# Inverse deviations and inverse lengths of a two-layer kernel: a root and a reciprocal, or a sum and a power on POOL

## The chip, the cores and the metric

The kernel runs on one core of one Trainium2 chip. A core has five engines with instruction queues of their own, each worked off in order: TensorE (PE, with its weight loads as PEld), VectorE (DVE), ScalarE (ACT), GpSimd (POOL) and SyncE (SP). Engines wait for each other on semaphores. The metric is the device time of one execution in microseconds (us), all of it: two layers of a small sequence model, 8 sequences of 512 tokens with 128 channels, in float32.

## The reference, cut to what matters

Every block is preceded by a normalisation with mean and deviation over the 128 channels (`_layernorm`), and adds its result to `x`.

```python
def _layernorm(x, axis=-1, eps=1e-05):
    m = jnp.mean(x, axis=axis, keepdims=True)
    v = jnp.var(x, axis=axis, keepdims=True)
    return (x - m) / jnp.sqrt(v + eps)
...
x = x + _L0_attn_ref(_layernorm(x, axis=-1), ...)
x = x + _L0_ffn_ref(_layernorm(x, axis=-1), ...)
x = x + _L1_attn_ref(_layernorm(x, axis=-1), ...)
x = x + _L1_ffn_ref(_layernorm(x, axis=-1), ...)
```

Inside the blocks there are more inverse roots. The first attention divides each query and key of 8 numbers (16 heads) by its length, and normalises its output:

```python
q = _l2norm((x @ Wq).reshape(b, s, nh, d))
k = _l2norm((x @ Wk).reshape(b, s, nh, d))
...
state = state * (1.0 - bb * kk) + bb * (vt[..., :, None] * kt[..., None, :])
out_t = jnp.einsum('bhij,bhj->bhi', state, qt)
...
out = (out - mu) / jnp.sqrt(var + LN_EPS) * ln_g + ln_b
```

The second attention normalises its input once more, divides each head of its output by the root of its mean square, and normalises again ahead of a small feed-forward part:

```python
h = _ln(x, ln_w, ln_b)
...
o = _rms(o, rms_w) * (g * jax.nn.sigmoid(g))
x = x + o.reshape(Bb, Tt, HEADS * DV) @ Wo
h2 = _ln(x, ln_w, ln_b)
return x + jax.nn.gelu(h2 @ W1 + b1, approximate=False) @ W2 + b2
```

Both feed-forward blocks are mixtures of experts: a router chooses 2 of 8 experts in the first layer and 4 of 16 in the second.

## The kernel before, in words

A batch is one sequence: `x_b` is a tile of 128 partitions by 4 times 128 channels (token 128 t + p lies in partition p, block t). A deviation is thus a number for each token: [128 x 4] for a batch. A length is one for each token and head: 128 x 4 x 32 numbers for queries and keys.

The work has five stages.

1. First attention and first router, for all eight batches (chains `attend0` and `route`, run by the planner at line 918). Tokens of a routed batch are scattered to DRAM row by row by POOL (line 839, eight indirect DMAs for each batch).
2. The eight experts of the first layer, in a fixed order (lines 937 to 970).
3. Second attention, its feed-forward part and second router (chain `attend`), again for eight batches; sixteen indirect DMAs for each batch (line 1413).
4. The sixteen experts of the second layer over 36 groups of four tiles of rows (`fetch`, `prepare`, `first`, `second`).
5. The sum of the four expert results into `x` and the store (lines 1629 to 1638).

In stages 1 and 3 the order of the instructions on each engine is found by a planner when the program is built. A chain is a generator; `yield ACT, 0.35, "sqrt"` says that the next instructions run on ACT, take 0.35 us, and need the table of that name. The planner (`Order.run`, line 143) always takes the step that can begin first by its own clock, on a tie the one with the lower rank (the lower batch). It knows that an engine does one thing at a time, a hop of 0.2 us between engines, and 1.3 us for a change of ACT's table. A chain also waits for signals of other chains and for buffers out of rings. Where PE would idle for more than 0.35 us by the planner's clock, it puts in fills: matmuls into a bank that nobody reads (line 907). The engines then run these lists in order, each instruction as soon as its semaphores allow. What the planner does not know is real: how long transfers take, and what other work an engine has outside the chains, such as the constants that POOL loads at the start (lines 188 to 326).

What the change touches:

- `statistics` (line 426): moments of `x` on DVE, root on ACT (436), reciprocal (438) and shift (439) on DVE, for batch 0, batches 1 and 2, and batches 3 to 7.
- `attend0`: sums of squares of queries and keys come out of PSUM at line 592, are inverted at 593, the root is taken by ACT at 598. Lines 601 and 602 make the factors `f`: [0:16] is (1 + th) / length squared of the key, [16:32] is (1 + th) / length of the key, [32:48] is 1 / length of the query; `th` is the tanh half of beta's sigmoid (595). The factors are transposed by PE (606), copied by ACT (609), and spread over the channels (613, 548, 502); keys, queries and values are multiplied with them (617, 551, 505).
- The recurrence runs on DVE in two groups of four numbers for each batch, over [128 x 2048]: products at 646, 652 and 662 and a scan at 658. ACT makes 1 - product at 626. The keys and queries for it are stored to DRAM and read back spread over partitions (lines 479 and 554).
- `deviation` (line 676): mean square of the result out of PSUM, root on ACT (687), reciprocal on DVE (690), used at 709.
- `route` (line 716): moments, root (725), reciprocal (727), shift (728), normalised rows on ACT (732).
- `attend`: three normalisations, called u, m and g, with roots at 1087 and 1088, at 1255, and at 1298, and the common `shifts` (line 1059, reciprocal at 1062); the head norm with its sum at 1222, root at 1224 and reciprocal at 1226.

Five batches of stage 3 may be in flight (`FLIGHT = 5`), four of stage 1.

Of the kernel before, what the change touches and what calls it, by code (L numbers as in the profile page):

```python
# [9 lines left out]
F32 = mybir.dt.float32  # L10
# [24 lines left out]
DV = 8  # L35
# [26 lines left out]
PE, DVE, ACT, POOL, SP = "PE", "DVE", "ACT", "POOL", "SP"  # L62
# [107 lines left out]
def two_layers(ctx: ExitStack, tc: tile.TileContext, a: dict, out: bass.AP):  # L170
    nc = tc.nc

    const = ctx.enter_context(tc.tile_pool(name="const", bufs=1))
# [35 lines left out]
    nc.gpsimd.affine_select(  # L209
        out=before, in_=ones, pattern=[[1, P]], compare_op=ALU.is_gt, fill=0.0, base=0, channel_multiplier=-1  # L210
    )
    eps = const.tile([P, 1], F32, name="eps")
    nc.vector.memset(eps, EPS)
    eps2 = const.tile([P, 1], F32, name="eps2")
    nc.vector.memset(eps2, EPS * EPS)
    over_c = const.tile([P, 1], F32, name="over_c")
    nc.vector.memset(over_c, 1.0 / C)
    center = const.tile([P, P], F32, name="center")
# [55 lines left out]
    ps = bank_ring.idle[0][2]  # L274
# [122 lines left out]
    mv_a = const.tile([P, B, NT, 2], F32, name="mv_a")  # L397
# [14 lines left out]
    def chunk(t2, t):  # L412
        return t2[:, t * P : (t + 1) * P]

    def affine(dst, src, rs, sh):
        for t in range(NT):
            nc.scalar.activation(
                dst[:, t, :], src[:, t, :], AF.Identity, bias=sh[:, t : t + 1], scale=rs[:, t : t + 1]
            )

    def landing(us):
        s = Signal()
        s.set(order.later(us))
        return s

    def statistics(first, last):

        yield landing(3.0 + first)
        for b in range(first, last):
            yield DVE, 1.75  # L430
            for t in range(NT):
                nc.vector.bn_stats(st_a[:, t, :], xs[b][:, t, :])
                nc.vector.bn_aggr(mv_a[:, b, t, :], st_a[:, t, :])
        yield ACT, 0.35, "sqrt"
        rs, sh = rs_a[:, first:last, :], sh_a[:, first:last, :]
        nc.scalar.activation(rs, mv_a[:, first:last, :, 1], AF.Sqrt, bias=eps)
        yield DVE, 0.4
        nc.vector.reciprocal(rs, rs)
        nc.vector.scalar_tensor_tensor(sh, mv_a[:, first:last, :, 0], -1.0, rs, ALU.mult, ALU.mult)
        for b in range(first, last):  # L440
            have_stats[b].set(order.now)

    def attend0(b):
# [3 lines left out]
        m = yield flight  # L447
# [3 lines left out]
        ps = yield bank_ring  # L451
# [112 lines left out]
        ps = yield bank_ring  # L564
# [17 lines left out]
        ps = yield bank_ring  # L582
# [5 lines left out]
        used_xT()  # L588
        sq_ring.give(order.now, *sq)
        by_kind = ps[:, : NT * 3 * NH].rearrange("p (t n) -> p t n", t=NT)  # L590
        yield DVE, 1.3
        nc.vector.tensor_scalar_max(m.norms, by_kind[:, :, 0 : 2 * NH], 1e-24)
        nc.vector.reciprocal(m.norms, m.norms)
        yield ACT, 0.25, "silu"
        nc.scalar.activation(m.th, by_kind[:, :, 2 * NH :], AF.Tanh, scale=0.5)
        bank_ring.give(order.now, ps)
        yield ACT, 0.4, "sqrt"
        nc.scalar.activation(m.f[:, :, NH:], m.norms, AF.Sqrt)

        yield DVE, 0.45  # L600
        nc.vector.scalar_tensor_tensor(m.f[:, :, 0:NH], m.th, 1.0, m.norms[:, :, 0:NH], ALU.add, ALU.mult)
        nc.vector.scalar_tensor_tensor(m.f[:, :, NH : 2 * NH], m.th, 1.0, m.f[:, :, NH : 2 * NH], ALU.add, ALU.mult)
        ps = yield bank_ring
        yield PE, 0.6
        for t in range(NT):
# [5 lines left out]
        ps = yield bank_ring  # L611
# [64 lines left out]
        def deviation():  # L676
            sq = yield sq_ring
            yield ACT, 0.65
            nc.scalar.activation(sq, acc, AF.Square)
            gone.set(order.now)  # L680
            ps = yield bank_ring
            yield PE, 0.7
            for t in range(NT):
                nc.tensor.matmul(ps[:, t : t + 1], lhsT=chunk(sq, t), rhs=over_c, start=True, stop=True)
            sq_ring.give(order.now, sq)
            yield ACT, 0.3, "sqrt"
            nc.scalar.activation(m.rs_o, ps[:, :NT], AF.Sqrt, bias=eps)
            bank_ring.give(order.now, ps)
            yield DVE, 0.15
            nc.vector.reciprocal(m.rs_o, m.rs_o)  # L690
            have_rs.set(order.now)

        order.add(b, deviation())
# [5 lines left out]
        ps = yield bank_ring  # L699
# [16 lines left out]
    def route(b):  # L716

        x_b = xs[b]
        m = yield routed
        yield DVE, 1.75  # L720
        for t in range(NT):
            nc.vector.bn_stats(m.st[:, t, :], x_b[:, t, :])
            nc.vector.bn_aggr(m.mv[:, t, :], m.st[:, t, :])
        yield ACT, 0.3, "sqrt"
        nc.scalar.activation(m.rs, m.mv[:, :, 1], AF.Sqrt, bias=eps)
        yield DVE, 0.3
        nc.vector.reciprocal(m.rs, m.rs)
        nc.vector.scalar_tensor_tensor(m.sh, m.mv[:, :, 0], -1.0, m.rs, ALU.mult, ALU.mult)
        rw_b = yield rows_ring
        yield ACT, 2.3  # L730
        for t in range(NT):
# [4 lines left out]
                bias=m.sh[:, t : t + 1],  # L736
                scale=m.rs[:, t : t + 1],
            )
        ps = yield bank_ring
# [20 lines left out]
        ps = yield acc_ring  # L760
# [59 lines left out]
        ps = yield bank_ring  # L820
# [233 lines left out]
    def moments(m, src, which):  # L1054
        for t in range(NT):
            nc.vector.bn_stats(m.st[:, t, :], src[:, t, :])
            nc.vector.bn_aggr(m.mv[which][:, t, :], m.st[:, t, :])

    def shifts(m, which, n):

        mv, rs, sh = m.mv[which], m.rs[which], m.sh[which]
        nc.vector.reciprocal(rs, rs)
        mean = mv[:, :, 0].unsqueeze(1).to_broadcast([P, n, NT]) if n > 1 else mv[:, :, 0].unsqueeze(1)
        nc.vector.scalar_tensor_tensor(sh, mean, -1.0, rs, ALU.mult, ALU.mult)

    def attend(b):
# [10 lines left out]
        m = yield flight  # L1077
# [5 lines left out]
        yield DVE, 1.75  # L1083
        moments(m, x_b, "u")

        yield ACT, 0.6, "sqrt"
        nc.scalar.activation(m.rs["u"][:, 0, :], m.mv["u"][:, :, 1], AF.Sqrt, bias=eps)
        nc.scalar.activation(m.rs["u"][:, 1, :], m.mv["u"][:, :, 1], AF.Sqrt, bias=eps2, scale=1.0 + EPS)
        yield DVE, 0.35
        shifts(m, "u", 2)  # L1090

        u = yield u_ring
# [16 lines left out]
        ps = yield bank_ring  # L1109
# [33 lines left out]
        ps = yield bank_ring  # L1143
# [76 lines left out]
        nc.scalar.activation(o, tiled(acc), AF.Square)  # L1220
        yield DVE, 0.7
        nc.vector.tensor_reduce(m.rr, o.rearrange("p t (h d) -> p (t h) d", d=DV), AX.X, ALU.add)
        yield ACT, 0.35, "sqrt"
        nc.scalar.activation(m.rr, m.rr, AF.Sqrt, bias=eps, scale=1.0 / DV)
        yield DVE, 1.3
        nc.vector.reciprocal(m.rr, m.rr)
        nc.vector.tensor_mul(
            o.rearrange("p t (h d) -> p (t h) d", d=DV),
            tiled(acc).rearrange("p t (h d) -> p (t h) d", d=DV),
# [3 lines left out]
        ps = yield bank_ring  # L1233
# [10 lines left out]
        ps = yield bank_ring  # L1244
# [6 lines left out]
        bank_ring.give(order.now, ps)  # L1251
        yield DVE, 1.75
        moments(m, u, "m")
        yield ACT, 0.3, "sqrt"
        nc.scalar.activation(m.rs["m"][:, 0, :], m.mv["m"][:, :, 1], AF.Sqrt, bias=eps)
        yield DVE, 0.35
        shifts(m, "m", 1)
        hn = yield hn_ring
        yield ACT, 1.65
        affine(hn, u, m.rs["m"][:, 0, :], m.sh["m"][:, 0, :])  # L1260
        ps = yield bank_ring
# [18 lines left out]
        ps = yield bank_ring  # L1280
# [13 lines left out]

        yield DVE, 1.75
        moments(m, x_b, "g")
        yield ACT, 0.3, "sqrt"
        nc.scalar.activation(m.rs["g"][:, 0, :], m.mv["g"][:, :, 1], AF.Sqrt, bias=eps)
        yield DVE, 0.35
        shifts(m, "g", 1)  # L1300
        rw_b = yield rows_ring
        yield ACT, 2.95
        for t in range(NT):
# [14 lines left out]
        ps = yield bank_ring  # L1318
# [52 lines left out]
        ps = yield bank_ring  # L1371
# [304 lines left out]
```

## Time and profile before

| | us |
|---|---|
| median of three runs | 1202.57 |
| lowest and highest | 1201.56, 1208.95 |
| profiled execution, its own time | 1211.52 |
| its span, first to last instruction | 1209.8 |

Busy time in that span: PE 943.3, PEld 680.0, DVE 658.2, ACT 474.7, POOL 448.0 us. ACT loads a table 81 times, at 1283 ns each: 33 times in stage 1, 47 in stage 3, once in stage 4.

| stage | from | to |
|---|---|---|
| 1 first attention and router | 0 | 404 |
| 2 first experts | 404 | 497 |
| 3 second attention and router | 497 | 894 |
| planning of the second experts, last scatters | 894 | 913 |
| 4 second experts | 913 | 1170 |
| 5 sum and store | 1170 | 1210 |

How to read it: a line of the timeline gives start, duration, engine, line of the kernel, operation, what is written from what with shapes, and in brackets how long the engine had been idle and what ended that. A line of the waits gives who waited for whom, the total, the number of times and the longest. In the table by stage each row gives the stretch, its length, then for PE, PEld, DVE, ACT and POOL the busy time with the number of instructions, then TensorE's granted clock, the share of the DMA engines and GB/s. "remote" and "issue" are idle times for which the profile shows no engine and no transfer as the cause.

### The profile page before, as it was taken

How to read it: one execution, taken by the hardware profiler on the slowest of the kernel's cores; microseconds unless marked ns; L12 is line 12 of the kernel's file. 1: busy time of each engine (PE TensorE's matmuls, PEld its weight loads, DVE VectorE, ACT ScalarE, POOL GpSimd, SP SyncE). 2: the span in 40 equal slices, each digit the busy share in tenths (PEclk: the TensorE clock that was granted, in tenths of full speed). 3: DMA queues.
4: the chain of work that ended last, by engine and by line, in shares of the span. 5: the costliest groups of instructions: out<-in, count | busy, mean ns of one | idle time of the engine just before them, and what ended most of it. 6: DMA issues, size and time to landing. Idle time of an engine off the chain costs nothing. (4 is left out here: it accounts for less than half of the span.)

```text
span 1209.8 us, 16157 instructions
## 1 busy us (share of the span) xinstructions
PE 943.3 (78%) x4923; PEld 680.0 (56%) x4923; DVE 658.2 (54%) x1628; ACT 474.7 (39%) x892; POOL 448.0 (37%) x459
## 2 busy tenths in 40 slices
PE   7989999997988499689977977977646778768620
PEld 5656566664657266555644544644535677757520
DVE  5478889777962011367766856654342333434317
ACT  4623664733432022272932843623402334333310
POOL 8000045314334234210055145134442656655543
PEclk8887888877977699889987978978867888888765
DMA  7866667585400200340012001001002222222228
GB/s 173 208 151 151 158 162 184 153 202 133 112 6 3 72 15 10 107 146 1 1 36 79 10 27 36 12 25 36 32 31 70 78 75 81 81 74 79 71 80 274
DMA packets 76438, 103.79 MB, mean 86 GB/s; under 512 B 12404, under 2 KB 58358, under 8 KB 72256
## 3 DMA queue, kind: packets, MB, share of 16 engines
q1 hardware_dynamic: 56576, 72.55, 23.4%
q0 software_dynamic: 14832, 27.84, 8.0%
q10 hardware_dynamic: 4944, 2.37, 0.7%
q8 instruction: 40, 0.66, 0.2%
q14 instruction: 46, 0.38, 0.1%
HBM read 69.63 MB, written 37.99 MB: 89 GB/s over the span
## 5 line engine op out<-in xcount | busy, mean ns | idle before, releaser
L839 POOL DMA_INDIRECT row<-rows,si x64 | 92.3, 1442 | 275.8 <-DVE kT L617 144.9
L1413 POOL DMA_INDIRECT rows<-rows,si x128 | 126.3, 986 | 166.0 <-DVE tmp L1390 69.1
L1597 POOL DMA_INDIRECT res<-qy,to x144 | 141.3, 981 | 118.4 <-DVE qw L1558 55.2
L1576 ACT ACTIVATE qh<-mid,cols 128x128 f32<-128x128 f32 x288 | 86.2, 365 | 144.0 <-PE qT L1553 59.8
L907 PEld LDWEIGHTS idle_bank<-ones,ident 128*128 128x128 f32 x956 | 130.9, 214 | 17.3 <-issue 14.6
L907 PE MATMUL idle_bank<-ones,ident 128*128 128x128 f32 x956 | 136.9, 299 | 3.3 <-POOL ident masks.py:199 1.5
L1568 PE MATMUL mid<-dT,qw 128*128 128x128 f32 x576 | 88.0, 315 | 7.9 <-issue 5.9
L1595 DVE TENSOR_TENSOR qy<-qyp,de 128x512 f32<-128x512 f32 x36 | 24.8, 690 | 127.3 <-PE qT L1553 54.3
L1568 PEld LDWEIGHTS mid<-dT,qw 128*128 128x128 f32 x576 | 84.2, 230 | 9.9 <-issue 7.7
L1587 PE MATMUL qyp<-fw,qh 128*128 x576 | 80.4, 291 | 11.8 <-issue 11.7
L1587 PEld LDWEIGHTS qyp<-fw,qh 128*128 128x128 f32 x576 | 75.4, 207 | 13.5 <-issue 12.5
L635 PE MATMUL acc<-add,center 128*128 128x512 f32 x128 | 68.4, 684 | 17.8 <-DVE add L662 17.6
L1553 PE MATMUL qT<-ident,de 128*128 128x128 f32 x144 | 33.2, 311 | 50.4 <-DMA de<-rows 35.1
L658 DVE TENSOR_TENSOR_SCAN add<-dec,add 128x2048 f32<-128x2048 f32 x16 | 70.8, 4424 | 0.6
L1558 DVE COPY qw<-fw 128x256 f32 x144 | 46.2, 336 | 22.8 <-DMA rows<-rows,si 9.8
L635 PEld LDWEIGHTS acc<-add,center 128*128 128x128 f32 x128 | 26.9, 220 | 50.3 <-issue 28.9
L963 POOL DMA_INDIRECT res<-y,de x32 | 31.3, 977 | 62.7 <-DVE y L957 55.4
L1553 PEld LDWEIGHTS qT<-ident,de 128*128 128x128 f32 x144 | 19.2, 149 | 62.2 <-issue 32.8
L943 ACT ACTIVATE hT<-mid,cols 128x512 f32<-128x512 f32 x32 | 22.0, 687 | 75.4 <-PE mid L940 50.8
L1103 POOL TENSOR_TENSOR x<-x,b 128x512 f32<-128x512 f32 x8 | 10.6, 1321 | 109.1 <-DVE u L1098 92.4
L662 DVE TENSOR_TENSOR add<-add,qb 128x2048 f32<-128x2048 f32 x16 | 36.6, 2288 | 23.9 <-DMA qb<-queries 23.6
L1186 PEld LDWEIGHTS acc<-ident,st 128*128 128x128 f32 x256 | 37.4, 216 | 20.3 <-issue 11.3
(338 smaller groups left out, 1949.6 us busy)
## 6 DMA issues: line engine op xcount, KB each, us to landing
add<-keys SPq DMA_DIRECT2D x16, 1024.0 KB
qb<-queries SPq DMA_DIRECT2D x16, 1024.0 KB
de<-rows SPq DMA_DIRECT2D x144, 65.0 KB
yk<-res SPq DMA_DIRECT2D x8, 1024.0 KB
res<-zeros POOLq DMA_DIRECT2D x8, 512.0 KB
ew_all<-in_L_ffn_ew_dram SPq DMA_DIRECT2D x16, 256.0 KB
ys<-res SPq DMA_DIRECT2D x8, 512.0 KB
fw<-in_L_ffn_w_dram SPq DMA_DIRECT2D x32, 128.0 KB
```

Of the source, the lines that this page charges most:

```text
L635: nc.tensor.matmul(acc, lhsT=center, rhs=st[:, j, :], start=g + j == 0, stop=(g + 1) * J + j == D + J - 1)
L658: nc.vector.tensor_tensor_scan(flat, dec.rearrange("p j t -> p (j t)"), flat, 0.0, ALU.mult, ALU.add)
L839: nc.gpsimd.indirect_dma_start(out=row0_w[(b * NT + t) * 2 + k], out_offset=bass.IndirectOffsetOnAxis(ap=m.si[:, t, k : k + 1], axis=0), i ...
L907: nc.tensor.matmul(idle_bank[:, 0:P], lhsT=ident, rhs=ones, start=True, stop=True)
L1186: nc.tensor.matmul(acc[:, t * P : (t + 1) * P], lhsT=st[:, t * P : (t + 1) * P], rhs=ident, start=j + t == 0, stop=j + t == DK + NT - 2,)
L1413: nc.gpsimd.indirect_dma_start(out=rows1_w[(b * NT + t) * K1 + k], out_offset=bass.IndirectOffsetOnAxis(ap=m.si[:, t, k : k + 1], axis=0), ...
L1553: nc.tensor.transpose(ps[:, i * P : (i + 1) * P], de[q][:, i, 0:C], ident)
L1558: nc.vector.tensor_copy(w1_q[:, i, :], fw1[:, bass.ds(at, I1)])
L1568: nc.tensor.matmul(mid[c][:, here], lhsT=w1_q[:, i, c * P : (c + 1) * P], rhs=dT[:, here], start=True, stop=True)
L1576: nc.scalar.activation(hT[:, c, here], mid[c][:, here], AF.Gelu, bias=cols[:, bass.ds(at + c, 1)])
L1587: nc.tensor.matmul(ps[:, here], lhsT=hT[:, c, here], rhs=fw2[:, bass.ds(at + c * C, C)], start=c == 0, stop=c == NC1 - 1,)
L1597: nc.gpsimd.indirect_dma_start(out=res1_w[4 * q + i], out_offset=bass.IndirectOffsetOnAxis(ap=to[:, i : i + 1], axis=0), in_=y[:, i, :], i ...
```

## The change

Every inverse root is taken on POOL as (a + more) to the power of -0.5, with at most two instructions: a sum (or a product and a sum) with numbers, and a power whose exponent is a constant column. ACT takes no square root any more, and DVE inverts none of these. [...]DVE brings them out first: the maximum at 592 as before, and at 687 a sum with EPS in place of ACT's root. The key's factor with the squared length is now made by a product with the inverse length once more, and (1 + th) / length is copied into its place. The planner's entries are changed along with it.

```diff
+    minus_half = const.tile([P, 1], F32, name="minus_half")
+    nc.vector.memset(minus_half, -0.5)
...
+    def root(dst, src, factor, more):
+
+        if factor == 1.0:
+            nc.gpsimd.tensor_scalar_add(dst, src, more)
+        else:
+            nc.gpsimd.tensor_scalar(dst, src, factor, more, ALU.mult, ALU.add)
+        power(dst, dst)
+
+    def power(dst, src):
+        half = minus_half
+        while len(half.shape) < len(src.shape):
+            half = half.unsqueeze(1)
+        nc.gpsimd.tensor_tensor(dst, src, half.to_broadcast(list(src.shape)), ALU.pow)
...
-        yield ACT, 0.35, "sqrt"
+        yield POOL, 0.7
         rs, sh = rs_a[:, first:last, :], sh_a[:, first:last, :]
-        nc.scalar.activation(rs, mv_a[:, first:last, :, 1], AF.Sqrt, bias=eps)
-        yield DVE, 0.4
-        nc.vector.reciprocal(rs, rs)
+        root(rs, mv_a[:, first:last, :, 1], 1.0, EPS)
+        yield DVE, 0.25
...
-        yield DVE, 1.3
+        yield DVE, 0.3
         nc.vector.tensor_scalar_max(m.norms, by_kind[:, :, 0 : 2 * NH], 1e-24)
-        nc.vector.reciprocal(m.norms, m.norms)
...
-        yield ACT, 0.4, "sqrt"
-        nc.scalar.activation(m.f[:, :, NH:], m.norms, AF.Sqrt)
+        yield POOL, 0.8
+        power(m.f[:, :, NH:], m.norms)
 
         yield DVE, 0.45
-        nc.vector.scalar_tensor_tensor(m.f[:, :, 0:NH], m.th, 1.0, m.norms[:, :, 0:NH], ALU.add, ALU.mult)
-        nc.vector.scalar_tensor_tensor(m.f[:, :, NH : 2 * NH], m.th, 1.0, m.f[:, :, NH : 2 * NH], ALU.add, ALU.mult)
+        r_k = m.f[:, :, NH : 2 * NH]
+        nc.vector.scalar_tensor_tensor(m.th, m.th, 1.0, r_k, ALU.add, ALU.mult)
+        nc.vector.tensor_mul(m.f[:, :, 0:NH], m.th, r_k)
+        nc.vector.tensor_copy(r_k, m.th)
...
-            yield ACT, 0.3, "sqrt"
-            nc.scalar.activation(m.rs_o, ps[:, :NT], AF.Sqrt, bias=eps)
+            yield DVE, 0.15
+            nc.vector.tensor_scalar_add(m.rs_o, ps[:, :NT], EPS)
             bank_ring.give(order.now, ps)
-            yield DVE, 0.15
-            nc.vector.reciprocal(m.rs_o, m.rs_o)
+            yield POOL, 0.4
+            power(m.rs_o, m.rs_o)
...
-        yield ACT, 0.3, "sqrt"
-        nc.scalar.activation(m.rs, m.mv[:, :, 1], AF.Sqrt, bias=eps)
-        yield DVE, 0.3
-        nc.vector.reciprocal(m.rs, m.rs)
+        yield POOL, 0.6
+        root(m.rs, m.mv[:, :, 1], 1.0, EPS)
+        yield DVE, 0.2
...
-        yield ACT, 0.6, "sqrt"
-        nc.scalar.activation(m.rs["u"][:, 0, :], m.mv["u"][:, :, 1], AF.Sqrt, bias=eps)
-        nc.scalar.activation(m.rs["u"][:, 1, :], m.mv["u"][:, :, 1], AF.Sqrt, bias=eps2, scale=1.0 + EPS)
-        yield DVE, 0.35
+        yield POOL, 1.0
+        root(m.rs["u"][:, 0, :], m.mv["u"][:, :, 1], 1.0, EPS)
+        root(m.rs["u"][:, 1, :], m.mv["u"][:, :, 1], 1.0 + EPS, EPS * EPS)
+        yield DVE, 0.2
         shifts(m, "u", 2)
...
-        yield ACT, 0.35, "sqrt"
-        nc.scalar.activation(m.rr, m.rr, AF.Sqrt, bias=eps, scale=1.0 / DV)
-        yield DVE, 1.3
-        nc.vector.reciprocal(m.rr, m.rr)
+        yield POOL, 0.8
+        root(m.rr, m.rr, 1.0 / DV, EPS)
+        yield DVE, 0.7
```

The roots of m and g change as that of u does, with one `root` each in place of ACT's root (`yield POOL, 0.6`), and `shifts` loses its reciprocal.

More of the change, by code (lines that the diff above doesn't have):

```diff
@@ L211, in two_layers @@
     )
[L212 to L215, printed above, removed]
+    minus_half = const.tile([P, 1], F32, name="minus_half")
+    nc.vector.memset(minus_half, -0.5)
     over_c = const.tile([P, 1], F32, name="over_c")
@@ L1061, in shifts @@
         mv, rs, sh = m.mv[which], m.rs[which], m.sh[which]
-        nc.vector.reciprocal(rs, rs)
         mean = mv[:, :, 0].unsqueeze(1).to_broadcast([P, n, NT]) if n > 1 else mv[:, :, 0].unsqueeze(1)
@@ L1253, in attend @@
         moments(m, u, "m")
-        yield ACT, 0.3, "sqrt"
-        nc.scalar.activation(m.rs["m"][:, 0, :], m.mv["m"][:, :, 1], AF.Sqrt, bias=eps)
-        yield DVE, 0.35
+        yield POOL, 0.6
+        root(m.rs["m"][:, 0, :], m.mv["m"][:, :, 1], 1.0, EPS)
+        yield DVE, 0.2
         shifts(m, "m", 1)
@@ L1296, in attend @@
         moments(m, x_b, "g")
-        yield ACT, 0.3, "sqrt"
-        nc.scalar.activation(m.rs["g"][:, 0, :], m.mv["g"][:, :, 1], AF.Sqrt, bias=eps)
-        yield DVE, 0.35
+        yield POOL, 0.6
+        root(m.rs["g"][:, 0, :], m.mv["g"][:, :, 1], 1.0, EPS)
+        yield DVE, 0.2
         shifts(m, "g", 1)
```

## The prediction

> **What bounds the kernel now.** I began with the page's first two parts and then cut the execution by stage, at the times where the first and last instruction of each stage's lines start. The table of busy time by stage, one row for each stretch (length, then busy time of PE, PEld, DVE, ACT, POOL with the number of instructions):
>
> ```profile
> 0.00:404.00 404.00, 350.16 (x1619) 242.07 (x1619) 282.12 (x596) 181.14 (x276) 124.35 (x131) 0.83 0.56 134
> 404.00:497.00 93.00, 86.78 (x455) 60.89 (x456) 11.07 (x16) 23.28 (x33) 30.66 (x32) 0.94 0.13 36
> 497.00:894.00 397.00, 317.84 (x1543) 204.68 (x1541) 243.13 (x712) 182.85 (x294) 125.80 (x132) 0.88 0.13 41
> 913.00:1170.00 257.00, 185.52 (x1296) 170.67 (x1296) 91.94 (x251) 87.47 (x289) 140.79 (x144) 0.84 0.26 71
> ```
>
> The edit lies in the first and third rows. PE looks busiest there, but 136.9 us of its time are the fills of L907, put where PE would idle. In the first stage the worker is DVE: from 57 to 366 us it is busy 247.6 of 309 us. In the third nothing is full (DVE 61%, ACT 46%, POOL 32%): chains of eight batches, five in flight, bound it. The chain that ended last reaches back only to about 907 us, so it says nothing of these two stages; the waits do. Table loads of ACT (line, count, busy time, mean ns):
>
> ```profile
> L598 ACT ACT_TABLE_LOAD x8 | 10.3, 1283 | 0.1
> L687 ACT ACT_TABLE_LOAD x3 | 3.8, 1283 | 0.1
> L1224 ACT ACT_TABLE_LOAD x6 | 7.7, 1283 | 0.1
> L1298 ACT ACT_TABLE_LOAD x6 | 7.7, 1283 | 0.1
> ```
>
> and DVE's longest waits in the first stage (waiter, awaited, total us, times, longest):
>
> ```profile
> DVE add L662 <- DMA qb<-queries: 23.6, 5, 8.3
> DVE lg L779 <- PE acc L765: 18.9, 3, 15.0
> DVE dec L656 <- ACT dec L626: 12.3, 4, 5.8
> ```
>
> ACT makes DVE wait for little: 12.3 us on `dec`, some 5 us elsewhere. That is the first warning that 68 us of loads are not 68 us of time.
>
> **What the Trainium skill says.** "ScalarE: Activation LUTs", What ACT_TABLE_LOAD costs: about 1283 ns a load and a drain of some 1380 ns. The trace agrees on the load (1283); the next ACTIVATE follows within 0.02 us, so I use 1.283 alone. "SBUF — State Buffer", Who interferes with whom: a DVE instruction with two SBUF inputs and a POOL instruction that reads SBUF exclude each other for the whole instruction. The trace shows both directions. The scatter that starts 1.1 us into a DVE scan takes 4.11 us instead of 0.98, and a shift of 0.17 us takes 1.00 beside POOL's add:
>
> ```profile
> 162.69 4.42 DVE L658 TENSOR_TENSOR_SCAN add<-dec,add 128x2048 f32<-128x2048 f32 x1
> 163.79 4.11 POOL L839 DMA_INDIRECT row<-rows,si  x1 [0.30 <-issue]
> ...
> 515.29 1.58 POOL L1103 TENSOR_TENSOR x<-x,b 128x512 f32<-128x512 f32 x1 [1.32 <-ACT h1T L1115]
> 515.89 1.00 DVE L1064 SCALAR_TENSOR_TENSOR sh_u<-mv_u,rs_u 128x8 f32<-128x8 f32 x1
> ```
>
> "GPSIMD Engine Reference", Elementwise, prices a two-input add at 2.6 cycles an element and gives no price for a power; L1103 (512 elements, 1.27 to 1.31 us undisturbed) fits the add.
>
> **The change part by part.** *Removed from ACT*: the changed program's order has 28 table loads for 81; 31 fewer in the first stage (33 to 2), 22 in the third (47 to 25). 53 x 1.283 = 68 us. The roots go too: 8 x (0.31 + 0.27 + 0.30) = 7 us in the first stage, 8 x (0.29 + 0.28 + 0.35 + 0.30 + 0.30) = 12 us in the third. ACT falls from 181 to about 134 and from 183 to about 143 us, beside the path wherever ACT waited anyway: several loads were issued while ACT still waited for its data (L1298: load at 755.47, root at 761.04).
>
> *Removed from and added to DVE*: first stage, 8 x (0.953 + 0.161 + 0.163) = 10.2 us of reciprocals; added 8 x 0.18 (sum out of PSUM, nearest row L828) and 8 x 0.20 (a copy of 64 elements, nearest L815 and L893) = 3.0. Net -7. Third stage, 8 x (0.547 + 0.192 + 0.165 + 0.158) = -8.5.
>
> *Added to POOL*: a power, not in the trace. Below, a POOL instruction of this size costs no less than the iota (0.16 to 0.28). Above, I let a power cost ten times the add per element (1.28/512 x 10 = 25 ns, an estimate): 3.2 us for 128 elements. I take the planner's own entries in the diff (0.8 for 128, 0.4 for 4, 0.2 for the sum), since its other entries match the trace (POOL 1.3 against 1.32 for L1103). That is 16.5 us in the first stage and 24 in the third, on a POOL that is busy 124 and 126 us.
>
> *The start.* The first root now stands in POOL's queue behind its constant loads, whose last begins at 19.47; before, ACT had it at 6.25. Working on: root about 20.6, shift 20.9, normalisation to 22.6, transposes, copy at about 24.0, against 18.77: +5. Then four loads (32.42, 33.96, 36.36, 39.80) vanish: -5. The first `kT` product stays at 44 to 45, but the second batch's factors come directly behind the first's, so its keys and queries leave earlier and DVE has work in the 8.3 us stall before 65.67: -4.
>
> *The middle* (57 to 366): DVE's work -6, half of its waits for `dec` -6. The lock: 8 x 1.8 us of POOL roots against a DVE that spends some 181 us of the stage (16 x 11.3) in instructions with two SBUF inputs. Half of a root on 60% of occasions delays DVE: 4 us; the dependent shift or factor that finds its root locked out behind a scan or product costs about 0.5 us for each batch: 4 more. Sum -4. *Its tail*: two loads in front of `rs_o` (356.31, 357.83) vanish: -3. First stage: -11.
>
> *The third stage*: DVE -8.5, half on the path: -4. DVE's waits for ACT there (o 14.3, gk 4.3, gate 4.2, rr 3.9) are 27 us; ACT loses a fifth of its load, and half of these waits: -12. Against that stands the queue. Scatters of one batch are 16 issues of 0.98 + 0.30 = 20.5 us, contiguous in the new order too; a later batch's root that becomes ready inside waits for their end. Laid on the old times, 8 of the roots after 606 us fall into such a block, waiting 17.8, 3, 8, 15, 1.4, 12.3, 18.3 and 16.3: 92 us. Queued behind such a root are shift, affine and transposes of that batch; four other batches cover it. I pass on a fifth: +18. Conversely roots put ahead of scatters hold them; the cover is the same. Third stage: +2.
>
> *Moved only*: at the end of that stage ACT's copy stalls for no engine or DMA that the profile shows, with the last but one block of scatters running:
>
> ```profile
> 881.19 0.59 ACT L1316 COPY xT<-bank 128x512 f32<-128x512 f32 x1 [14.83 <-remote]
> ```
>
> All of it is on the path. ACT's list is 120 rows shorter in the new order, so where such a stall falls is drawn anew; a third of it: -5. The expert stages are untouched; their stalls of 7 to 10 us ("remote") may shift, taken as zero, +-8.
>
> Sum: -11 + 2 - 5 = -14 us. It is made against the profiled execution (span 1209.8, 1.7 us around it, 1211.5 in all); the three runs have a median of 1202.57, and I set it off from that: 1202.6 - 14 = 1189, own range 1176 to 1201.
>
> **The rivals.** *Freed ACT counts fully*: all 27 and 12.3 us of waits vanish, the query stalls (23.6) halve, roots slip between scatters: first stage -26, third -24 = -50, 1152. For it: loads sit between steps of one chain in both stages. Against it: DVE's waits for ACT are small, and four fifths of the first stage's middle are DVE's own work.
>
> *POOL's queue becomes the bound (slower)*: half of the 92 us reaches the end: +46 instead of +18, the stall of 14.8 is not won, and the other gains stay (-11 - 16): +19, 1222. It decides from the point where more than 27/92 = 29% is passed on. For it: the new order fills PE 31 times more in the third stage (269 against 238 fills), most of them in one place ahead of the last routings, where roots stand behind scatters. Against it: five batches in flight.
>
> *The power is dear*: 3.2 us for 128 elements, 1.6 for 64: +2.4 and +1.0 for each batch on the factor and rms chains, holding DVE's two-input work out meanwhile: 8 x 3.4 = +27, less half for cover, on top of -14 and a little longer small roots: about 1203.
>
> That the change does not do what it says is excluded by the order: the square roots and their loads are gone.
>
> **How the numbers follow.** Forecast 0.42, full gain 0.20, queue 0.26, dear power 0.12. About 1% is what a measurement of this kernel can tell from no change, so 1190.5 and 1214.6 are the bounds. Faster: 0.25 of the forecast, all 0.20 of the full gain, 0.02 of the power = 0.47. Slower: 0.20 of the queue, 0.07 of the power = 0.27. Within: 0.26. The range leaves out a tenth at each side: 1152 to 1224.
>
> **What would show it.** Right: 28 loads; ACT busy near 390 us, DVE near 643, POOL near 488; first root of POOL at 20 us; first stage ending near 393, third about as long as now. Power of 4, 64 and 128 elements near 0.4, 0.6 and 0.8 us, those inside a DVE scan stretched to its end. Wrong: power rows over 2 us; roots of the third stage that start 10 us after their moments with scatters in between, and a third stage over 410 us; or DVE gaps in the first stage under 20 us in sum, which is the full gain.

## The result and the profile after

| | before | after |
|---|---|---|
| median, us | 1202.97 | 1460.51 |
| runs | 4 (1201.56 to 1208.95) | 4 (1459.84 to 1472.18) |
| profiled span, us | 1209.8 | 1458.0 |

The ratio is 1.2146, with a 95% interval of 1.2104 to 1.2188: the change makes the kernel 21% slower. The prediction (1189, range 1152 to 1224) was wrong.

The busy time by stage of the kernel after, cut where its own stages end (stretch, length, then PE, PEld, DVE, ACT, POOL with instructions, granted clock, DMA share, GB/s):

```profile
0.00:562.00 562.00, 365.75 (x1599) 251.20 (x1599) 276.91 (x585) 133.24 (x218) 328.60 (x169) 0.73 0.40 98
562.00:655.00 93.00, 89.30 (x482) 63.62 (x482) 11.02 (x16) 21.98 (x32) 31.07 (x32) 0.97 0.12 35
655.00:1145.00 490.00, 348.74 (x1549) 225.32 (x1550) 239.59 (x679) 145.58 (x232) 249.98 (x211) 0.79 0.10 32
1162.00:1418.00 256.00, 186.40 (x1298) 171.65 (x1298) 94.17 (x258) 87.27 (x289) 140.73 (x145) 0.85 0.26 72
```

The expert stages are as long as before (93 and 256 us). From DVE's first instruction of one stage's lines to that of the next, the first stage takes 562 us in place of 410, and the third, to the start of its last scatter, 506 in place of 406: +152 and +99 of the span's +248. DVE and ACT do no more work than before in either; POOL does 204 and 124 us more. The groups of POOL that are new (line, operation, written from read, shapes, count, then busy us and mean ns of one, then idle time before them):

```profile
L431 POOL TENSOR_TENSOR f<-norms,minus_half 128x128 f32<-128x128 f32 x8 | 165.8, 20732 | 15.5 <-DVE norms L603 14.4 <-DVE rs_o L699 1.0
L431 POOL TENSOR_TENSOR rr<-rr,minus_half 128x64 f32<-128x64 f32 x8 | 84.2, 10523 | 0.7
L431 POOL TENSOR_TENSOR rs_g<-rs_g,minus_half 128x4 f32<-128x4 f32 x8 | 8.4, 1045 | 0.7
L431 POOL TENSOR_TENSOR rs_m<-rs_m,minus_half 128x4 f32<-128x4 f32 x8 | 8.3, 1038 | 0.7
```

A power costs 1.04, 10.5 and 20.7 us for 4, 64 and 128 elements in each partition: a straight line of 0.16 us an element with 0.4 us ahead of it. And DVE waits for it. Its longest waits in the first stage of the kernel after (waiter, awaited, total us, times, longest):

```profile
DVE th L612 <- POOL f L431: 159.5, 8, 27.3
DVE lg L790 <- PE acc L776: 18.4, 3, 15.0
```

and in its third stage:

```profile
DVE o L1236 <- POOL rr L431: 69.2, 8, 11.0
DVE add L1214 <- remote: 28.4, 3, 12.9
```

Before, the longest of DVE's waits in the first stage was 23.6 us in all. 159.5 is close to the stage's +152, and 69.2 is most of the third's +99. One batch, the third, and what follows it in the timeline:

```profile
138.85 20.73 POOL L431 TENSOR_TENSOR f<-norms,minus_half 128x128 f32<-128x128 f32 x1 [12.78 <-DVE norms L603]
...
140.29 0.26 DVE L603 TENSOR_SCALAR norms<-bank 128x128 f32<-128x128 f32 x1
...
159.57 0.23 POOL L422 TENSOR_SCALAR rs<-mv 128x4 f32<-128x4 f32 x1
159.61 0.23 DVE L612 SCALAR_TENSOR_TENSOR th<-th,f 128x64 f32<-128x64 f32 x1 [19.07 <-POOL f L431]
...
161.72 20.76 POOL L431 TENSOR_TENSOR f<-norms,minus_half 128x128 f32<-128x128 f32 x1
...
163.69 0.57 ACT L621 COPY fT<-bank 48x512 f32<-48x512 f32 x1
...
182.52 0.23 DVE L612 SCALAR_TENSOR_TENSOR th<-th,f 128x64 f32<-128x64 f32 x1 [21.32 <-POOL f L431]
...
204.86 0.22 DVE L612 SCALAR_TENSOR_TENSOR th<-th,f 128x64 f32<-128x64 f32 x1 [20.83 <-POOL f L431]
...
207.80 0.68 DVE L629 TENSOR_TENSOR kT<-kT,bank 128x512 f32<-128x512 f32 x1
```

DVE has brought out two batches' sums of squares by 140.55, and the next instruction in its list is the factor `th` of the first of them. It stands still for 19 us until the power ends. The recurrences of the first two batches are over by then, and that of the third needs these factors. But when they are there, and their transposed copy too (164.26), the third batch's first product `kT` still does not begin: it stands in DVE's list behind two more waits of 21 us, for the powers of later batches, and comes at 207.80. In this trace not one of the recurrence's 64 products and scans runs beside a power of the lengths. A small root of `route` (159.57) whose moments were there at 140 waits behind the power as well.

Of the table loads what was planned came about: 28 remain (two of the rows), none of them for a root.

```profile
L1174 ACT ACT_TABLE_LOAD x6 | 7.7, 1283 | 0.1
L1286 ACT ACT_TABLE_LOAD x6 | 7.7, 1283 | 0.1
```

### The profile page after: what moved, and what is told of

Same layout as the page of the kernel before. It is cut to its first block, busy times and chain, and to the rows that moved or that the text cites. A ratio compares the mean times of both kernels' runs of the same rounds, so it can differ in the third digit from the quotient of the medians.

```text
span 1458.0 us, 16173 instructions
## 1 busy us (share of the span) xinstructions
PE 994.9 (68%) x4961; PEld 715.5 (49%) x4961; DVE 650.4 (45%) x1584; ACT 388.6 (27%) x772; POOL 776.2 (53%) x577
## 4 chain that ended last, share of the span: by engine, by line
issue 31%; PE 15%; POOL 5%; DVE 5%; DMA 3%; SPq 2%; another core or an unknown queue 1%; ACT 0%; DVEq 0%; POOLq 0%
PE mid L1577 5%; PE qyp L1596 4%; POOL rr L431 2%; DMA yk<-res 1%; POOL res L974 1%; SPq L1556 1%; PE qT L1562 1%; DVE x L1644 1%; PE bank L1187 1%; PE acc L1196 1%; POOL rs_u L431 1%; PE bank L1185 1%; POOL res L1606 1%; DMA de<-rows 0%
## 5 line engine op out<-in xcount | busy, mean ns | idle before, releaser
L431 POOL TENSOR_TENSOR f<-norms,minus_half 128x128 f32<-128x128 f32 x8 | 165.8, 20732 | 15.5 <-DVE norms L603 14.4
L918 PE MATMUL idle_bank<-ones,ident 128*128 128x128 f32 x994 | 155.5, 311 | 18.3 <-issue 15.7
L918 PEld LDWEIGHTS idle_bank<-ones,ident 128*128 128x128 f32 x994 | 146.0, 224 | 40.4 <-issue 37.5
L850 POOL DMA_INDIRECT row<-rows,si x64 | 97.9, 1530 | 107.1 <-issue 48.3
L431 POOL TENSOR_TENSOR rr<-rr,minus_half 128x64 f32<-128x64 f32 x8 | 84.2, 10523 | 0.7
L612 DVE SCALAR_TENSOR_TENSOR th<-th,f 128x64 f32<-128x64 f32 x8 | 2.0, 249 | 159.5 <-POOL f L431 159.5
L763 PE MATMUL bank<-xT,rw 128*128 128x512 f32 x64 | 38.2, 729 | 33.3 <-ACT th L605 18.3
L1187 PE MATMUL bank<-h1T,wqs 128*128 128x512 f32 x64 | 43.8, 772 | 15.7 <-DVE add L1214 15.5
L1196 PE MATMUL acc<-ident,st 128*128 128x128 f32 x256 | 41.6, 315 | 13.7 <-DVE st L1222 12.5
```

The lines of the kernel that those rows point to most:

```text
L431: nc.gpsimd.tensor_tensor(dst, src, half.to_broadcast(list(src.shape)), ALU.pow)
L850: nc.gpsimd.indirect_dma_start(out=row0_w[(b * NT + t) * 2 + k], out_offset=bass.IndirectOffsetOnAxis(ap=m.si[:, t, k : k + 1], axis=0), i ...
L918: nc.tensor.matmul(idle_bank[:, 0:P], lhsT=ident, rhs=ones, start=True, stop=True)
L1187: nc.tensor.matmul(qj, lhsT=wqs[:, j, :], rhs=hT, start=True, stop=True)
L1196: nc.tensor.matmul(acc[:, t * P : (t + 1) * P], lhsT=st[:, t * P : (t + 1) * P], rhs=ident, start=j + t == 0, stop=j + t == DK + NT - 2,)
```

## The experiments

My theory after the result, A: the powers' duration is the loss, because DVE, working its list in order, stands behind each long one. Rivals: B, the roots' place in POOL's queue (behind scatters) and the mutual exclusion of POOL and DVE cost the time; C, the order is bad because the planner was told 0.8 us for what takes 20.7.

The runs fell on different chips. On that of the first four the kernel before takes 1195 us, on those of the others 1070, and the traces taken on the latter have none of the idle time called "remote", which on DVE alone is 72 us in the trace of before. Every ratio below is to the kernel before on the same chip, and differences in us are compared within one kind of chip only.

### Additions in place of powers

The order of every engine stays that of the changed kernel; an addition of the same form takes the place of the power, for the lengths, for the head norms, and for all but the norm `m`. What is computed is then no inverse root, and tokens may be routed otherwise; the expert stages take about as long all the same (93 us, and 232 from the first to the last scatter of the second experts, against 93 and 234 in the changed kernel).

```diff
-        power(m.f[:, :, NH:], m.norms)
+        power(m.f[:, :, NH:], m.norms, ALU.add)
...
```

> In this kernel only the power over the 128 lengths of a batch (row f) becomes an addition of the same form on POOL; the lengths are then no inverse roots, all else and every engine's order stay as in the changed kernel. Theory A (the changed kernel pays the duration of the long powers, and DVE stands still behind them): each row f falls from 20.7 us to under 0.8, the first stage comes back by about 150 us from 563 to 410, the third stage stays at about 496 long: 1460 - 152 = about 1305 (1290 to 1320). Rival B (the roots' place in POOL's queue and their mutual exclusion with DVE cost the time, whatever the power takes): under half comes back, above 1380.

> Only the power over the 64 head norms of a batch (row rr) becomes an addition of the same form on POOL. Theory A: each row rr falls from 10.5 us to under 0.6, and DVE's waits of 69 us for it vanish; the scatters behind it on POOL start earlier by the same amount, so 70 to 90 us of the third stage's extra 99 come back and the first stage stays at 563: about 1380 (1365 to 1395). Rival B (the third stage's extra time is that of roots queued behind blocks of scatters): under 40 us come back, above 1420.

> Every power except the one of the normalisation ahead of the gelu (m) becomes an addition of the same form on POOL; the order of every engine stays that of the changed kernel, so what is left is the change at the price of a cheap instruction. Theory A: the whole loss was the price, and the step list of the forecast is tested as it stands: first stage about 393 long, third about 400, 1190 to 1215 in all. Rival B (queue, order and exclusion): above 1240, the third stage over 430 long although no power is in it but m.

Measured: 1304.28 us without the power of the lengths (ratio 1.0946, 1.0894 to 1.0998), 1365.91 without that of the head norms (1.1459, 1.1395 to 1.1522), 1208.33 without all but `m` (1.0120, 1.0067 to 1.0173). The first stage returns to 417 us with the first edit, the third from 506 to 421 with the second. The two groups of the first edit's kernel, and that of the head norms in the second's:

```profile
L431 POOL TENSOR_TENSOR rr<-rr,minus_half 128x64 f32<-128x64 f32 x8 | 84.2, 10524 | 0.7
L431 POOL TENSOR_TENSOR f<-norms,minus_half 128x128 f32<-128x128 f32 x8 | 3.2, 404 | 27.3 <-DVE norms L603 27.3
...
L431 POOL TENSOR_TENSOR rr<-rr,minus_half 128x64 f32<-128x64 f32 x8 | 2.3, 292 | 0.7
```

The same form over the same 128 elements takes 0.40 us as an addition and 20.7 as a power: it is the power that is dear, not the broadcast exponent or the engine. The granted clock, 0.73 in the first stage of the changed kernel against 0.83 before, is 0.84 there with the first edit: the lower clock came with the power too. In the order of the changed kernel, then, A holds and B fails as an account of the 21%. But the third kernel is slower than the one before by 1.2%, where my forecast for a cheap power was a gain: its first stage takes 416 us, where A had it near 393, its third 417. That remained to be explained.

### What the table loads are worth

The kernel before, with an identity of the same scale and bias in place of each root on ACT (no root is taken), first in the unchanged order of every engine, then in the order that the planner draws when told that no table is needed.

```diff
-        nc.scalar.activation(m.f[:, :, NH:], m.norms, AF.Sqrt)
+        nc.scalar.activation(m.f[:, :, NH:], m.norms, AF.Identity)
...
```

> The kernel before, its order kept on every engine, with each root on ACT replaced by an identity with the same scale and bias, so that ACT loads no table for it (about 30 loads in place of 81); the deviations and lengths are then squares. It measures what the vanished loads are worth without POOL. By the recorded steps (loads beside the path for the most part): the waits for ACT halve, 10 to 25 us under the kernel before. Rival 'freed ACT counts fully': 40 to 60 us under it. If the loads are wholly beside the path: within 8 us of it.

> As the one before it, but the planner too is told that the root needs no table, and draws a new order. If order matters little: within 10 us of the one before it. If the freedom to put roots anywhere is worth more than the loads: 15 us or more under it.

Measured: 1073.26 us against 1070.40, ratio 1.0014 (0.9991 to 1.0037); with the new order 1115.65, ratio 1.0411 (1.0353 to 1.0469). Fifty table loads (81 before, 31 here) are worth nothing that can be measured on this chip: they lay beside the path. On a chip of the other kind, where the forecast was made, this was not run. And a new order alone loses 4%, with the same instructions in the chains; only the fills on PE are more.

### How much the draw of an order is worth

The kernel before with the planner's hop between engines at 0.21 or 0.19 us in place of 0.20. The work is the same; fills and table loads follow the order.

```diff
-HOP = 0.2
+HOP = 0.21
```

> The kernel before with the planner's hop between engines at 0.21 us in place of 0.20: not one instruction of the chains is another, only the order is drawn anew. If the order of the kernel before is one of many equals: within 1% of it. If it is a good draw, as the 4% lost by a new order without table loads suggest: 1.01 to 1.05 of it.

> The same with a hop of 0.19 us, a third draw of the order. Equals: within 1% of the kernel before. A good draw before: 1.01 to 1.05 of it.

Measured: 1.0069 (1.0038 to 1.0099) and 1.0369 (1.0298 to 1.0440). The order of the kernel before is the best of these three, and a change that makes the planner draw anew can lose up to 4% for no reason of its own. With three draws I can't say how good the kernel's own is among many.

### POOL's queue without a new order

The additions once more, but with the planner's entries of the kernel before, so that the order is drawn with roots on ACT and their tables, while sums and additions are issued on POOL where it plans those.

```diff
-        yield POOL, 0.8
+        yield ACT, 0.4, "sqrt"
         power(m.f[:, :, NH:], m.norms, ALU.add)
...
```

> The instructions of the kernel with additions in place of all powers but m, in the order that the planner draws with the entries of the kernel before: it plans ACT roots with their tables, and POOL's sums and additions are put where it plans them. If the 1.2% by which that kernel was slower than the one before were a worse order: 0.995 to 1.005 of the kernel before. If they were POOL's queue and the mutual exclusion of POOL and DVE, which are the same here: 1.01 or more. By the recorded forecast (the change pays at a cheap power): 0.98 to 0.99.

Measured: 1094.43 us, ratio 1.0189 (1.0119 to 1.0259), some 20 us. The first stage is 400.1 us long, against 400.7 in the kernel with identities; the third 357.8 against 338.1. The first stage is equal and all of the loss lies in the third, where DVE waits for roots that take 0.2 to 0.5 us (1.04 for `m`, which is still a power). Its longest waits there:

```profile
DVE o L1236 <- POOL rr L431: 12.6, 4, 4.9
DVE sh_g L1074 <- POOL rs_g L431: 10.8, 4, 4.4
DVE x L1091 <- DMA ys<-res: 10.5, 1, 10.5
DVE sh_m L1074 <- POOL rs_m L431: 9.9, 7, 3.3
```

What stands ahead of the root in the longest of these waits (POOL and DVE alone, earlier scatters left out):

```profile
788.63 0.97 POOL L1422 DMA_INDIRECT rows<-rows,si  x1 [0.30 <-issue]
789.91 0.97 POOL L1422 DMA_INDIRECT rows<-rows,si  x1 [0.30 <-issue]
790.95 0.24 POOL L424 TENSOR_SCALAR rr<-rr 128x64 f32<-128x64 f32 x1
791.27 0.29 POOL L431 TENSOR_TENSOR rr<-rr,minus_half 128x64 f32<-128x64 f32 x1
791.60 0.69 DVE L1236 TENSOR_TENSOR o<-acc,rr 128x512 f32<-128x512 f32 x1 [4.90 <-POOL rr L431]
```

The sum over the head was ready at 786.70; the root takes 0.6 us and begins 4.3 us later, behind scatters. All eight of the waits for a root that last over 2 us (26 us together) have scatters directly ahead of the root. So roots on POOL do cost something in the stage with sixteen scatters a batch, and POOL's queue is seen in these waits. How the 20 us divide between the queue, the extra hop between two engines, the exclusion of POOL and DVE and the power of `m`, no run separates.

### Only the small roots on POOL

Lengths and head norms go back to ACT and DVE; the roots of 4 numbers stay on POOL. Three plans: the changed kernel's entries, real durations, and the entries of the kernel before.

```diff
-        yield POOL, 0.8
-        power(m.f[:, :, NH:], m.norms)
+        yield ACT, 0.4, "sqrt"
+        nc.scalar.activation(m.f[:, :, NH:], m.norms, AF.Sqrt)
...
```

> The lengths f and the head norms rr go back to ACT's root and DVE's reciprocal as before; only the roots of 4 numbers for each partition (and the three of the statistics) stay on POOL, as sum and power of about 1.04 us. The planner draws a new order. Theory A: no long power is left, so the time is that of the kernel before within the scatter of a new order, with the small powers 0.6 us longer than planned: 1195 to 1235. Rival B (small roots queued behind scatters are what costs): the third stage stays over 450 long, above 1270.

> Lengths and head norms on ACT and DVE as before, roots of 4 numbers on POOL, with the planner told their real duration (1.1 to 2.7 us, 1.1 to 5.9 for the statistics). With the planner's low entries this kernel was 41 us slower than the one before. If those 41 us come from a plan made with too short powers: within 15 us of the kernel before. If they come from POOL's queue (roots behind blocks of scatters, which the planner does know): still 30 us or more slower.

> Lengths and head norms by ACT and DVE as before, roots of 4 numbers on POOL, in the order drawn with the entries of the kernel before. With redrawn orders this took 1.038 and 1.066 of the kernel before. If the order was the cause: 1.00 to 1.015. If POOL's queue is (a root of 1 us waits for a block of scatters): 1.02 or more, with the third stage 10 us or more longer than that of the kernel before and the first stage about equal.

Measured: 1235.79 us, ratio 1.0376 (1.0324 to 1.0429); 1144.07 us, 1.0661 (1.0595 to 1.0727); 1120.37 us, 1.0451 (1.0407 to 1.0496). The first is just above what A allowed. In the third, where the plan is the old one, the first stage is 414.6 us (14 over the kernel with identities) and the third 368.5 (30 over it). No new order is needed for this loss, then: roots of about 1 us on POOL lose 4.5% in the order of the kernel before. The queue alone, as I had put it, is not the account either, since it was to leave the first stage about equal; with additions, in the same order, it is (400.1), with powers of 1.04 us it is 14 us longer. With none of these plans do roots of about 1 us on POOL pay, and real durations in the planner did not mend it. How much the draw adds or takes in the other two can't be said with these runs.

### Is it the duration or the plan?

The changed kernel's instructions, with planner's entries nearer to what POOL took (12 or 13 us for the lengths, 10.9 for the head norms, 1.1 to 5.9 for the rest), and with those of the kernel before; the changed kernel itself beside them on the same chip. An entry of 20.8 us, what the power of the lengths takes, gives no order: the chains then wait for each other in the planner.

```diff
-        yield POOL, 0.8
+        yield POOL, 13
         power(m.f[:, :, NH:], m.norms)
...
-        yield POOL, 0.8
+        yield POOL, 10.9
         root(m.rr, m.rr, 1.0 / DV, EPS)
...
```

> The changed kernel with the planner told what POOL's roots took on the chip: 12 us for the power of the lengths (of 20.7; from 14 us on the chains block each other in the planner), 10.9 for the head norms, 1.1 to 2.7 for roots of 4 numbers, 1.1 to 5.9 for the statistics. The instructions are the same ones. Theory A: the power stands in every batch's chain and is paid per element, so another order hides only a part of it: 1.14 to 1.22 of the kernel before. Rival C (the loss is that of a plan made with wrong prices; a right plan covers the powers with other batches' work): under 1.10.

> The changed kernel once more, beside a plan with longer entries on the same chip. If the loss is a sum of durations that nothing hides, it is the same number of us on any chip: the kernel before plus 245 to 270 us, which is 1.24 where that takes 1070 us and 1.21 where it takes 1200.

> The changed kernel with the planner told 13 us for the power of the lengths, 10.9 for the head norms, 1.1 to 5.9 for the rest. Theory A alone (the duration, whatever the order): within 3 points of the changed kernel on the same chip. With C as a second cause: 1.11 to 1.15 of the kernel before, thus 80 us or more under the changed kernel on the same chip.

> The changed kernel's instructions, powers and all, in the order that the planner draws with the entries of the kernel before (roots on ACT, with tables). Its entries for the roots are as short as those of the changed kernel. If short entries are what makes an order bad for long powers: within 3 points of the changed kernel. If the changed kernel's own draw was unlucky: 5 points or more under it.

| plan, same instructions | us | over before | ratio (95%) | first stage | third stage |
|---|---|---|---|---|---|
| changed kernel | 1357.01 | +287 | 1.2662 (1.2612 to 1.2712) | 554.8 | 465.0 |
| entries of the kernel before | 1265.54 | +196 | 1.1800 (1.1746 to 1.1853) | 486.0 | 446.4 |
| 12 us for the lengths | 1212.64 | +142 | 1.1295 (1.1218 to 1.1372) | 477.0 | 399.1 |
| 13 us for the lengths | 1202.94 | +133 | 1.1237 (1.1188 to 1.1285) | 466.1 | 399.4 |

(The kernel before took 1070.33 us beside the third row, 1069.82 beside the others.) A alone fails: it expected the 13-us plan within 3 points of the changed kernel, and they are 14 apart; it also had the changed kernel at +245 to +270 on this chip, and it takes +287. C alone, which put the 12-us plan under 1.10, fails too. The order is thus a second cause beside the duration: with another one, 154 of the 287 us go. How much of that is the wrong price is not settled. The old plan, whose entries are about as blind to the power's length, is 9 points (91 us) under the changed kernel's, so the latter was also an unlucky draw; 63 us more separate the old plan from the 13-us plan, most of them in the third stage, where DVE waits 85.6 us for the head norms with the one and 12.6 with the other. What the price in the plan is worth lies between 63 and 154 us, as far as four orders can tell. DVE's longest wait in the first stage of the changed kernel on this chip:

```profile
DVE th L612 <- POOL f L431: 158.3, 8, 27.3
```

and its waits in the first stage of the 13-us plan:

```profile
DVE th L612 <- POOL f L431: 46.4, 6, 15.4
DVE lg L790 <- PE acc L776: 21.1, 3, 11.7
DVE kT L629 <- PE bank L625: 16.4, 3, 11.0
DVE x L721 <- POOL rs_o L431: 16.3, 4, 11.1
```

POOL does the same powers (165.8 and 165.7 us for the lengths), but 112 us of the waiting for them are gone, and in the third stage the wait for the head norms falls from 76.3 to 12.6 us. The timeline of the 13-us plan shows what took the place of the gap of 19 us above:

```profile
106.89 20.72 POOL L431 TENSOR_TENSOR f<-norms,minus_half 128x128 f32<-128x128 f32 x1
116.94 0.69 DVE L629 TENSOR_TENSOR kT<-kT,bank 128x512 f32<-128x512 f32 x1 [10.96 <-PE bank L625]
117.66 2.29 DVE L658 TENSOR_TENSOR dec<-add,kT 128x2048 f32<-128x2048 f32 x1
...
120.91 2.28 DVE L674 TENSOR_TENSOR add<-add,qb 128x2048 f32<-128x2048 f32 x1
123.11 2.28 DVE L658 TENSOR_TENSOR dec<-add,kT 128x2048 f32<-128x2048 f32 x1
125.42 2.29 DVE L664 TENSOR_TENSOR add<-add,vT 128x2048 f32<-128x2048 f32 x1
```

While one batch's power runs, DVE works on another's recurrence, here after a wait of 11 us for PE. In the whole first stage of this plan 20 of the recurrence's products and scans lie wholly beside a power of the lengths, against none in the changed kernel. What stays, 133 us, is what this plan can't cover. In the first stage the start is a part of it: three powers run there in a row, from 34.3 to 96.4 us, and the first product `kT` comes at 59.51 us, against 43.09 in the kernel with identities. No plan tried, and no division of the roots, comes to the kernel before.

## Why the prediction was wrong, by its own steps

**The price of the power: the step that failed.** "Above, I let a power cost ten times the add per element ... 3.2 us for 128 elements. I take the planner's own entries." The power takes 20.73 us, 26 times the value taken and 6.5 times the upper bound. The bound had no ground: nothing in the trace of before spoke of a power, and ten times an addition was a guess dressed as an estimate; against the addition of the same form (0.40 us) the power is 51 times. That the planner's other entries match their instructions was no evidence for these. With the measured durations in the same sum, the powers put 166 + 84 us into the chains, against the 13 planned for the two: enough to see that the forecast can't hold. The prediction's own signs of being wrong, power rows over 2 us and a third stage over 410 us, both came.

**"The power is dear": the right rival, mis-sized.** It named the mechanism at 0.12 chance and priced it at 3.2 us, +27 less half for cover. At 20.7 and 10.5 us the planned cover was not half but none: the waits for `f` (159.5 us) are more than the first stage's gain in length.

**The planner's entry as a mere number.** I used the entries as prices, and missed their second role: they set DVE's order. With a short entry the consumer stands directly behind its producer. The same powers cost 287 us in the changed kernel's order and 133 in the 13-us plan's, though 91 us of that difference go with an order from other short entries too.

**Table loads.** 28 remain, as forecast, and ACT's busy time is 388.6 us (forecast near 390). But the gains that I let them bring (half of DVE's waits for ACT, -12 in the third stage, and the shares in the first) measure as zero, 1.0014, on a chip of the other kind. The warning that I wrote down, that 68 us of loads are not 68 us of time, should have been taken to its end. "Freed ACT counts fully" falls with it.

**The start.** Right in its first half: POOL's first sum begins at 19.13 us, and the first copy at 22.97 in place of 18.77 (+4; forecast +5). The -5 and -4 that should follow did not. Of the four loads only three vanish, since the gates need their table still (a load at 42.30; the prediction's own count of two left in this stage includes it). With additions the second batch's factors come directly behind the first's, as said, but the first `kT` product is at 47.34 us, not at 44 to 45, and the stall of 8.3 us is there as before (7.96, at 69.81).

**The queue.** The forecast's +18 for the third stage is close to what its own experiment shows, 19.7 us with cheap roots in the old plan; the rival's +46 is not. That is luck in part: the fifth that is passed on was a guess, the 92 us were laid on the old times, and the 19.7 us were measured on a chip of the other kind and are not all queue. What failed, as far as the runs show, is the other side of the sum, the gains that this was to offset. Additions end 1.2% slower rather than at -14 us: the profiled first stage is 6 us longer than before and the third 10. How that divides on those chips, between queue, order and idle time called "remote", is not shown.

**The lock.** Partly wrong. A power that begins inside a product of DVE with two inputs is held up, as forecast (the product lasts from 122.90 to 125.18, the power of 1.04 us takes 3.01):

```profile
122.90 2.28 DVE L674 TENSOR_TENSOR add<-add,qb 128x2048 f32<-128x2048 f32 x1
123.07 3.01 POOL L431 TENSOR_TENSOR rs_o<-rs_o,minus_half 128x4 f32<-128x4 f32 x1 [40.85 <-DVE rs_o L699]
```

But a power under way does not hold DVE: the products in the timeline of the 13-us plan take their 2.28 to 2.29 us, as without one. The Trainium skill ("SBUF — State Buffer", Who interferes with whom), on which the step rested, says that a DVE instruction with two SBUF inputs contends with a GpSimd instruction that reads SBUF, and calls the contention an exclusive lock; that the first holds the ports for the whole instruction it says of DVE's two-port modes, and the prediction carried it over. This run shows no such lock by a power under way, and the measurement decides. "Half of a root on 60% of occasions delays DVE" has no counterpart for the powers.

**The rest.** DVE's busy time is 650.4 us (forecast 643). The stall of 14.83 us at a copy of ACT is gone from that place, but idle time called "remote" stands before other instructions, such as the 28.4 us of `add` above; on DVE it sums to 118 us, against 72 before: redrawn, not won. POOL's 776.2 us against a forecast of 488 is the price again.

## What to carry to other kernels

An operation that the profile has never shown needs a bound that can be defended, and where none is to be had, the range must say so; a measurement of one such instruction would have given the price. Whether an engine's freed time counts is read from who waits for it, and waits of 4 us at a time in a kernel whose engines run ahead may be worth nothing. Where an order is planned from prices, a wrong price can cost twice: once as duration, once as a plan that puts the consumer where it must wait; and a redrawn order by itself moved this kernel by 0.7 to 4%, so a small edit that redraws it is best compared in a kept order too.

## What the runs showed of the hardware that I had not expected

- A power on POOL costs 0.16 us for each element of a partition, with about 0.4 us ahead of them (1.04, 1.66, 3.55, 10.5 and 20.7 us for 4, 8, 20, 64 and 128 elements, all over 128 partitions), while an addition of the same form takes 0.20 to 0.22 us for 4 to 20 and 0.40 for 128. The Trainium skill ("GPSIMD Engine Reference", Elementwise) prices the addition alone.
- DVE's products and scans with two inputs run at full speed beside a power under way (16 products at 2.28 to 2.29 us and four scans at 4.42 in the 13-us plan); a power that begins inside one waits (3.01 us in place of 1.04).
- The same kernel takes 1195 to 1203 us on some chips and 1070 on others. The idle time called "remote" (72 us on DVE and 74 on ACT in the trace of before) is absent from the traces taken on the latter. The changed kernel, traced on both, has about the same first stage (562.0 and 554.8 us), but a third of 506 and 465 us and second experts of 234 and 184 us from the first to the last scatter. What that idle time is, the profile does not say.
